# Shift transposes as 64-row pairs at the head of a unit, and V and x work kept to one whole-array stretch, in an attention and FFN kernel

## The chip, the cores and the metric

The kernel runs on one core of a Trainium2 chip. The metric is the device time of one launch in microseconds (us); several runs are given by their median. One run was also recorded by the hardware profiler, and its span, from the first to the last instruction, is what the trace describes. The engines are named as the profile names them: PE is the matrix engine and PEld its weight loads, DVE the vector engine, ACT the scalar (activation) engine, POOL the GpSimd engine, SP the queue that issues DMAs.

## What is computed

A block of attention and a feed-forward block, both between layer norms, for 2 batches of 2048 tokens with 256 features, 16 heads of 64, and 768 hidden units. All data is float32.

```python
x = x + layernorm(attn(layernorm(x)))
x = x + layernorm(ffn(layernorm(x)))

def attn(x):                       # 16 heads, K = 64
    q, k, v = x @ Wq + bq, x @ Wk + bk, x @ Wv + bv
    p = softmax(q @ k.T / sqrt(K))
    y = x + (p @ v) @ Wo + bo
    return layernorm(y, eps=1e-3) * gamma + beta

def ffn(x):                        # weights are int32, scaled by 1/127
    return (silu(x @ wg.T) * (x @ wu.T)) @ wd.T
```

## The kernel before

**Units.** The attention is cut into 64 units `(b, p, c)`: 2 batches, 8 pairs of heads, 4 chunks of 512 queries, in this order. A unit has 16 key tiles `kt` of 128 keys, taken as two blocks, j = 0 and j = 1, of 8. For a key tile, `scores` (L581) makes four pairs of matmuls; one matmul of a pair works for each head, on 64 of the array's 128 rows. The first three pairs are the product of K and Q, each split in a rounded part and a rest. The fourth pair adds the softmax's shift: `unit` times `SH[u]`, a row of 512 numbers for each head. ACT then takes the exponent (L598). So the fourth pair can't start before `SH[u]` is there.

**Where the shift comes from.** While unit u's scores run, `max_pair` (L549) computes the raw scores of the next unit, one pair of matmuls between two key tiles, and DVE reduces them to maxima. `shift_min` (L568) leaves the negated maxima, by query, in `n8`. `shift_row` (L573) turns them: four transposes on the PE, into PSUM, and one ACT copy (L579) from there to `SH[u]` in SBUF.

**A unit's order** is written out by hand in `run_unit` (L791), and each engine works through its own instructions in that order. A block is: 8 key tiles of scores; one half of an earlier unit's output projection, `wo_half` (L232), on 64-row tiles; `add_up`, which sums exponents on DVE and POOL; `advance("R")`, which gives loads, norms and casts their turn; in block j = 0 then `advance("F")`, the work that uses the whole 128 by 128 array; then `pv` (L617), 16 matmuls with V on tiles of 64 columns. In block j = 0 a sum over the exponents (`sum_up`, L188) follows, on the same 64-column tiles. In block j = 1 there follow `shift_row` of the next unit, `cs_item` (L218), and a second `advance("F")`. `cs_item` adds the two halves of P times V on DVE (`cf`, L221), rounds the result on ACT (`cs`, L223) and leaves the rest of it to POOL (L224). The four transposes of `shift_row` use the whole array.

**Work for later** is handed out by `items` (L635). A job is a generator that yields "R" or "F", the kind of turn at which it wants to go on. `now(j, ...)` puts a piece into the "F" turn of block j. The pieces that matter here are:

- `projs` (L502): one or two projections of Q or K, 6 matmuls each, read out by ACT and DVE. A unit with c = 3 has three of them.
- `v_tile` (L527): 24 matmuls that make V for 512 keys and two head pairs, read out by one DVE add (L547).
- `next_x` (L494): loads a chunk of the next batch's x, normalizes it (ACT) and transposes it (`x_item`, L483).
- the `piece` jobs of `prep_jobs` (L322): transpose 18 pieces of the FFN's weights, one for each unit from the fifth on.
- `head_job` (L269): the norms between attention and FFN for batch 0, with 8 transposes at their end.

**PSUM.** All of `scores`, `wo_half`, `shift_row`, `projs`, `v_tile`, `x_item` and the transposes of jobs take their output buffers from one ring of two, `t`. `max_pair` and `pv` share another ring of two. A buffer is taken again when its readers are done.

Of the kernel before, what the change touches and what calls it, by code (L numbers as in the profile page):

```python
# [8 lines left out]
F32 = mybir.dt.float32  # L9
# [7 lines left out]
P = 128  # L17
# [11 lines left out]
def kernel(  # L29
# [18 lines left out]
    nc = tc.nc  # L48
# [105 lines left out]
    def double():  # L154

        return banks["t"].tile([P, 2, 512], F32, tag="t", name="t")
# [165 lines left out]
    def prep_jobs():  # L322
        jobs = []

        def piece(w, dst, o, i0):
            src = hd.tile([P, TT, D], F32, tag="hx", name="wi")[:, 0, :].bitcast(I32)
            nc.sync.dma_start(out=src, in_=w[o * P : (o + 1) * P, i0 * P : (i0 + 2) * P])
            yield "R"
            f = hd.tile([P, TT, D], F32, tag="hy", name="wf")[:, 0, :]
            nc.scalar.copy(f, src)  # L330
            yield "F"
            yield "F"
            ps = double()[:, 0, :]
            for i in range(2):
                nc.tensor.transpose(ps[:, i * P : (i + 1) * P], f[:, i * P : (i + 1) * P], ident)
            t = hd.tile([P, TT, D], F32, tag="ht", name="wt")[:, :2, :].bitcast(F32R)
            split(t, ps[:, : 2 * P])
            for k in range(2):
                nc.sync.dma_start(
                    out=dst[:, k, i0 : i0 + 2, o * P : (o + 1) * P],  # L340
                    in_=f32(t[:, k, :]).rearrange("p (i n) -> p i n", i=2),
                )

        for w, dst, no, ni in (
            (w_gate, wg_dram, HC, DC),
            (w_up, wu_dram, HC, DC),
            (w_down, wd_dram, DC, HC),
        ):
            for o in range(no):
                for i0 in range(0, ni, 2):  # L350
                    jobs.append(piece(w, dst, o, i0))
        return jobs
# [36 lines left out]
    with ExitStack() as actx:  # L389
# [76 lines left out]
        def x_load(b, c):  # L466
            t = hd.tile([P, TT, D], F32, tag="ht", name="xc")
            nc.sync.dma_start(out=t, in_=x_chunk(b, c))
            return t
# [23 lines left out]

        def next_x(b, c):  # L494

            t = x_load(b, c)
            yield "R"
            x_norm(b, c, t)
            yield "F"
            x_item(c, t)  # L500
# [71 lines left out]

        def shift_row(u):  # L573

            ps = double()[:, 0, :]
            for qt in range(QT):
                nc.tensor.transpose(ps[:, qt * P : (qt + 1) * P], n8[:, qt, :], ident)  # L577
            SH[u] = bw.tile([P, QB], F32R, tag="sh", name="sh", bufs=2)
            nc.scalar.copy(SH[u], ps)  # L579

        def scores(u, kt):  # L581

# [52 lines left out]
        def items(g):  # L635

            b, p, c = units[g]
            at = {}

            def put(j, kind, f, *a, late=False):  # L640
                at.setdefault((j, kind), []).append((late, lambda: f(*a)))

            def now(j, f, *a):


                def job():
                    f(*a)
                    yield from ()

                put(j, "F", job)  # L650

            left = len(units) - g
            if p == 0:
                put(1, "R", start_acc, c)
            if b == 0 and p and prep:
                put(0, "R", lambda: prep.pop(0), late=True)
            if b == 1 and 4 * p + c in (5, 11, 17, 23):
                put(0, "R", head_job, 0, (5, 11, 17, 23).index(4 * p + c), nc.gpsimd, late=True)
            if left == 3:
                put(1, "R", load_ffn, 0)  # L660
            if left == 2:
                put(0, "R", load_ffn, 1)
                put(1, "R", load_ffn, 2)
            if left == 1:
                put(0, "R", load_ffn, 3)
            if b == 0 and p == 0:

                put(0, "R", x_stats_item, 1, c, late=True)


            want = [(0, *units[g + 2])] if left > 2 else []
            nb, npair = (b, p + 1) if p + 1 < NP else (b + 1, 0)
            if nb < B:
                same = nb == b
                want += [
                    (1, nb, npair, i)
                    for i in {1: (0,) if same else (), 2: (1,) if same else (0, 1), 3: (2, 3)}.get(c, ())
                ]
            for i in range(0, len(want), 2):
                now(0, projs, *want[i : i + 2])  # L680
            if c == 0 and p % 2 == 0:

                if g:
                    now(0, v_tile, b, p // 2, 3)
            if nb == B:
                return at
            if c == 0:
                put(0, "R", load_w, 1, nb, npair)
            if c == 1:
                put(0, "R", load_w, 0, nb, npair)  # L690
            if c == 2:
                put(0, "R", load_wo, nb, npair)
            if nb != b and c < 2:
                put(0, "R", next_x, nb, 2 * c)
                put(1, "R", next_x, nb, 2 * c + 1)
            if npair % 2 == 0:
                pg = npair // 2
                if c == 0:
                    put(1, "R", load_wv, nb, pg)
                if c == 2:  # L700
                    now(1, v_tile, nb, pg, 0)
                if c == 3:
                    now(1, v_tile, nb, pg, 1)
                    now(1, v_tile, nb, pg, 2)
            return at

        def begin():


            first = units[0]  # L710
            xs = [acc[:, c * TT : (c + 1) * TT, :] for c in range(NC)]

            def raw(tag):
                return lambda: hd.tile([P, TT, D], F32, tag=tag, name="raw").rearrange(
                    "p t d -> p (t d)"
                )[:, :512]

            ws = [load_w(0, 0, 0), load_w(1, 0, 0, raw("hx")), load_wv(0, 0, raw("hy"))]
            for c in range(NC):
                nc.sync.dma_start(out=xs[c], in_=x_chunk(0, c))  # L720
                if c < 3:
                    next(ws[c])

            def stats(c):
                ln_stats([xs[c][:, i, :] for i in range(TT)], mvx[0], c * TT)

            def rstd(c, n, eng=None):
                k = slice(c * TT, (c + n) * TT)
                ln_rstd(rsx[0][:, k], nbx[0][:, k], mvx[0][:, k, :], n * TT, LN_EPS, eng)

            def maxima(a, b):
                for i in range(a, b):
                    max_pair(first, i)

            stats(0)
            rstd(0, 1)
            drain(ws[0])
            x_norm(0, 0, xs[0])
            drain(ws[1])
            stats(1)  # L740
            rstd(1, 1, nc.gpsimd)
            stats(2)
            x_item(0, xs[0])
            x_norm(0, 1, xs[1])
            stats(3)
            rstd(2, 2, nc.gpsimd)
            projs((0, *first))
            projs((1, 0, 0, 0))
            maxima(0, 2)
            x_item(1, xs[1])  # L750
            maxima(2, 3)
            x_norm(0, 2, xs[2])
            projs((1, 0, 0, 1))
            maxima(3, 5)
            x_item(2, xs[2])
            drain(ws[2])
            x_norm(0, 3, xs[3])
            maxima(5, 6)
            projs((1, 0, 0, 2))
            maxima(6, 8)  # L760
            x_item(3, xs[3])
            maxima(8, 9)
            projs((1, 0, 0, 3))
            maxima(9, 10)
            v_tile(0, 0, 0, True)
            maxima(10, 12)
            projs((0, *units[1]))
            maxima(12, 13)
            v_tile(0, 0, 1, True)
            maxima(13, 15)  # L770
            v_tile(0, 0, 2, True)
            maxima(15, 16)
            shift_min(first)
            v_tile(0, 0, 3, True)
            shift_row(first)
            drain(load_wo(0, 0))

        running = []
# [11 lines left out]

        def run_unit(g, u):  # L791
            at = items(g)
            ahead = units[g + 1] if g + 1 < len(units) else None
            behind = units[g - 1] if g else None
            for j in range(2):
# [23 lines left out]
                if j == 0:  # L819
                    if behind:  # L820
                        sum_up(behind, pvs[u][:, 1, :])
                    first_half(u, behind)
                else:
                    if ahead:
                        shift_row(ahead)
                    cs_item(u)
                    advance("F", at.get((j, "F"), []))

        with tc.manual_schedule(engines={EV.PE, EV.DVE, EV.Activation, EV.Pool}):
            begin()  # L830
# [285 lines left out]
```

## Time and profile before

| What | us |
|---|---|
| median of 3 runs (lowest, highest) | 3004.85 (3004.0, 3007.09) |
| profiled execution, device time | 3004.34 |
| its span | 3002.6 |
| DVE busy (71%) | 2131.2 |
| ACT busy (49%) | 1473.3 |
| POOL busy (82%) | 2454.2 |

The device time is 1.74 us more than the span. The mean granted clock of the PE is 0.991 of full speed. A unit takes about 42 us; the first unit's scores begin at about 58 us, the last unit ends at about 2733 us, and the FFN follows. In the groups of the profile a line shows the source line, the engine and the operation, the tiles written and read, the shapes, and after the bar the busy time, the mean length of one in ns, and the time its engine stood idle ahead of it with what ended that. In the timeline a line is one merged stretch: start, length, engine, line, operation, tiles, count, and in brackets the idle time ahead and its releaser. Matmuls overlap each other, so the distance from one weight load to the next says more of the PE's pace than the length of a matmul.

### The profile page before, as it was taken

To read this page: it belongs to the slowest core of one execution; us is meant where nothing else is said; L and a number is where in the kernel's file an instruction comes from. 1 tells how busy PE (TensorE), PEld (TensorE's weight loads), DVE (VectorE), ACT (ScalarE), POOL (GpSimd) and SP (SyncE) were. 2 spreads that over 40 slices of the span, in tenths; PEclk is the share of its full clock that TensorE was granted. 3 is DMA by queue.
4 is the path that set the end of the run, shared out by engine and by line. 5 is a ranking of instruction groups with operands and counts; after the bars stand their busy time and mean duration, and the time that the engine had idled before them with its cause. 6 is when DMAs were issued, how large, how long until landed. Compare 5 with 4: busy or idle time off the path is not lost. (4 is left out here: it accounts for less than half of the span.)

```text
span 3002.6 us, 48405 instructions
## 1 busy us (share of the span) xinstructions
PE 2902.3 (97%) x19236; PEld 1751.5 (58%) x19236; DVE 2131.2 (71%) x2755; ACT 1473.3 (49%) x1756; POOL 2454.2 (82%) x1451
## 2 busy tenths in 40 slices
PE   7999999999999999999999999999999999999787
PEld 5555555556555665556555665556555655556666
DVE  6777667676767777766777777776777777764775
ACT  4555445444544545564545545554554545444343
POOL 4999778787878788877888998898899889996553
PEclk9999999999999999999999999999999999999989
DMA  5000000000000000010100010000001001021100
GB/s 85 19 12 13 13 14 13 14 15 13 12 15 21 15 5 6 10 40 24 27 5 4 5 39 7 1 16 30 5 5 40 4 3 36 15 69 59 43 19 25
DMA packets 127475, 61.08 MB, mean 20 GB/s; under 512 B 77264, under 2 KB 120528, under 8 KB 126864
## 3 DMA queue, kind: packets, MB, share of 16 engines
q1 hardware_dynamic: 127088, 57.72, 7.7%
q8 instruction: 150, 2.46, 0.4%
q14 instruction: 77, 0.63, 0.1%
q0 software_dynamic: 160, 0.27, 0.1%
HBM read 39.85 MB, written 17.83 MB: 19 GB/s over the span
## 5 line engine op out<-in xcount | busy, mean ns | idle before, releaser
L615 POOL TENSOR_TENSOR accs<-accs,pt 128x1024 f32<-128x1024 f32 x636 | 1623.7, 2553 | 288.0 <-ACT pt L598 242.8
L566 DVE TENSOR_REDUCE nm<-s 128x2 f32<-128x1024 f32 x1024 | 1215.1, 1225 | 495.4 <-PE s L559 495.1
L598 ACT ACTIVATE pt<-t 128x1024 f32<-128x1024 f32 x1024 | 1049.7, 1027 | 254.2 <-PE t L597 193.9
L597 PE MATMUL t<-QN,KT 64*128 64x512 f32 x6144 | 912.6, 401 | 9.4 <-DVE hn L178 5.1
L625 PE MATMUL s<-pt,v 128*64 128x512 f32 x4096 | 910.5, 597 | 0.0
L597 PEld LDWEIGHTS t<-QN,KT 64*128 64x128 f32 x6144 | 520.7, 185 | 245.0 <-ACT pt L598 170.8
L625 PEld LDWEIGHTS s<-pt,v 128*64 128x64 f32 x4096 | 283.7, 137 | 541.1 <-issue 528.8
L559 PE MATMUL s<-KT,QN 64*128 64x512 f32 x2048 | 423.5, 410 | 3.7 <-DVE cf L221 1.9
L597 PE MATMUL t<-sh,unit 64*128 64x512 f32 x2048 | 405.3, 392 | 0.0
L615 POOL TENSOR_TENSOR accs<-accs,two 128x1024 f32<-128x1024 f32 x128 | 305.0, 2383 | 19.0 <-DVE two L608 9.1
L606 DVE TENSOR_TENSOR two<-pt 128x1024 f32<-128x1024 f32 x128 | 298.1, 2329 | 0.0
L559 PEld LDWEIGHTS s<-KT,QN 64*128 64x128 f32 x2048 | 192.0, 184 | 127.1 <-issue 62.7
L214 ACT COPY rr<-s 128x1024 f32<-128x1024 f32 x63 | 63.9, 1014 | 397.6 <-PE s L190 390.4
L579 ACT CAST sh<-t 128x512 fp32r<-128x512 f32 x64 | 37.6, 587 | 413.3 <-PE t L577 413.3
L254 DVE SCALAR_TENSOR_TENSOR acc<-t,rc,acc 128x256 f32<-128x256 f32 x500 | 206.9, 477 | 19.6 <-PE t L243 12.8
L597 PEld LDWEIGHTS t<-sh,unit 64*128 64x128 f32 x2048 | 192.9, 184 | 44.8 <-ACT sh L579 0.2
L612 POOL TENSOR_TENSOR accs<-pt 128x1024 f32<-128x1024 f32 x64 | 153.6, 2401 | 49.1 <-ACT pt L598 48.9
L512 PE MATMUL t<-xh,wqk 128*128 128x512 f32 x512 | 181.5, 415 | 12.3 <-ACT pt L598 10.1
L943 POOL TENSOR_TENSOR hT<-hf,hT 128x512 fp32r<-128x512 f32 x48 | 62.0, 1291 | 103.5 <-ACT hT L942 103.4
L512 PEld LDWEIGHTS t<-xh,wqk 128*128 128x128 f32 x512 | 97.7, 191 | 47.1 <-ACT pt L598 22.9
L522 ACT ACTIVATE QN<-t,bq_sb 128x512 fp32r<-128x512 f32 x64 | 44.0, 688 | 163.9 <-PE t L512 163.9
L221 DVE TENSOR_TENSOR cf<-s,rr 128x512 f32<-128x512 f32 x64 | 44.2, 691 | 104.2 <-PE s L625 104.2
(160 smaller groups left out, 2316.2 us busy)
## 6 DMA issues: line engine op xcount, KB each, us to landing
few<-rr SPq DMA_DIRECT2D x512, 0.5 KB, 2.0
xc<-in_L_attn_x_dram SPq DMA_DIRECT2D x8, 512.0 KB, 3.9
acc<-in_L_attn_bo_dram SPq DMA_DIRECT2D x8, 512.0 KB, 8.5
xT_dram<-hn SPq DMA_DIRECT2D x16, 256.0 KB, 2.9
out_dram<-o SPq DMA_DIRECT2D x15, 256.0 KB, 2.1
xT<-xT_dram SPq DMA_DIRECT2D x3, 1024.0 KB, 5.9
attn_dram<-acc SPq DMA_DIRECT2D x5, 512.0 KB, 2.6
acc<-in_L_attn_x_dram SPq DMA_DIRECT2D x4, 512.0 KB, 7.5
```

The costliest lines, as they stand in the source:

```text
L214: nc.scalar.copy(r, ps)
L254: nc.vector.scalar_tensor_tensor(a, ps[e][:, i * D : (i + 1) * D], inv[:, e, q : q + 1], a, ALU.mult, ALU.add)
L512: nc.tensor.matmul(ps[:, k, :], w[:, wi, dc, :], xx[:, dc, s], start=n == 0, stop=n == 5)
L559: nc.tensor.matmul(s[:, e, :], QN[u][half(e), 0, qt * P : (qt + 1) * P], KT[b, p, kc][half(e), 0, :], start=True, stop=True,)
L566: nc.vector.tensor_reduce(nm[u][:, :, qt, kc : kc + 1], s, AX.X, ALU.max, negate=True)
L597: nc.tensor.matmul(ps[:, e, :], w, r, start=n == 0, stop=n == 3)
L598: nc.scalar.activation(pt, ps, AF.Exp, scale=QSCALE)
L606: nc.vector.tensor_tensor(two, p8[n], p8[n + 1], ALU.add)
L612: nc.gpsimd.tensor_tensor(accs[u], todo[0], todo[1], ALU.add)
L615: nc.gpsimd.tensor_tensor(accs[u], accs[u], t, ALU.add)
L625: nc.tensor.matmul(pvs[u][half(e), 0, :], v[:, kt % 4, n : n + K], pt[:, e, :], start=kt % 8 == 0, stop=kt % 8 == 7,)
L943: nc.gpsimd.tensor_tensor(t[:, 1], hf, f32(t[:, 0]), ALU.subtract)
```

## The change

`shift_row` moves from the end of a unit, for the next one, to the head of the unit that uses it; so in program order it now stands behind the `cs_item` of the unit before, and no longer ahead of it. Its transposes are now eight on halves of the array, one for each of the two 64-row tiles in turn, with 64 columns of the identity each; the two tiles write to the two halves (banks) of the `t` buffer, and the ACT copy puts the halves together with strided patterns. For the first unit it moves behind the load of the first `wo`.

The second "F" turn, at the end of block j = 1, is gone. What stood there goes into block j = 0: V tile 0 of the next two head pairs into the unit with c = 2, tiles 1 to 3 together into the unit with c = 0 that first uses them (tile 3 was there already), and the transposes of `next_x` and of `head_job` into the next "F" turn of a block j = 0. `next_x` uses three buffers in turn, so that two chunks can be loaded in the same turn. A weight `piece` yields "F" once, which leaves it in the same stretch as before, and except for p = 1 no piece starts in a unit with c = 2.

```diff
@@ piece @@
             yield "F"
-            yield "F"
             ps = double()[:, 0, :]
@@ next_x @@
-            t = x_load(b, c)
+            t = hd.tile([P, TT, D], F32, tag=("hx", "hy", "ht", "hx")[c], name="xc")
+            nc.sync.dma_start(out=t, in_=x_chunk(b, c))
@@ shift_row @@
-            ps = double()[:, 0, :]
+            ps = double()
             for qt in range(QT):
-                nc.tensor.transpose(ps[:, qt * P : (qt + 1) * P], n8[:, qt, :], ident)
+                for h in range(2):
+                    nc.tensor.transpose(
+                        ps[:, h, qt * K : (qt + 1) * K], n8[half(h), qt, :], ident[half(h), half(h)]
+                    )
             SH[u] = bw.tile([P, QB], F32R, tag="sh", name="sh", bufs=2)
-            nc.scalar.copy(SH[u], ps)
+            nc.scalar.copy(
+                SH[u].rearrange("p (q h r) -> p h q r", h=2, r=K),
+                ps[:, :, : QT * K].rearrange("p h (q r) -> p h q r", r=K),
+            )
@@ items (now() has no j any more: always block 0) @@
-            if b == 0 and p and prep:
+            if b == 0 and p and (c != 2 or p == 1) and prep:
...
-                if g:
-                    now(0, v_tile, b, p // 2, 3)
+                for i in range(1, 4) if g else ():
+                    now(v_tile, b, p // 2, i)
...
-                put(1, "R", next_x, nb, 2 * c + 1)
+                put(c, "R", next_x, nb, 2 * c + 1)
...
                 if c == 2:
-                    now(1, v_tile, nb, pg, 0)
-                if c == 3:
-                    now(1, v_tile, nb, pg, 1)
-                    now(1, v_tile, nb, pg, 2)
+                    now(v_tile, nb, pg, 0)
@@ begin @@
             v_tile(0, 0, 3, True)
-            shift_row(first)
             drain(load_wo(0, 0))
@@ run_unit @@
             at = items(g)
+            shift_row(u)
...
                 else:
-                    if ahead:
-                        shift_row(ahead)
                     cs_item(u)
-                    advance("F", at.get((j, "F"), []))
```

More of the change, by code (lines that the diff above doesn't have):

```diff
@@ L641, in put, with now @@
                 at.setdefault((j, kind), []).append((late, lambda: f(*a)))
-            def now(j, f, *a):
+            def now(f, *a):
                 def job():
@@ L648, in job @@
                     yield from ()
-                put(j, "F", job)
+                put(0, "F", job)
             left = len(units) - g
@@ L679, in items @@
             for i in range(0, len(want), 2):
-                now(0, projs, *want[i : i + 2])
+                now(projs, *want[i : i + 2])
             if c == 0 and p % 2 == 0:
-                if g:
-                    now(0, v_tile, b, p // 2, 3)
+                for i in range(1, 4) if g else ():
+                    now(v_tile, b, p // 2, i)
             if nb == B:
```

## The prediction, made before the changed kernel ran

> **What bounds the kernel now.** I read the page's busy times and slices first, then the groups, then the timeline of one seam between two units, then the list of waits.
>
> ```profile
> span 3002.6 us, 48405 instructions
> PE 2902.3 (97%) x19236; PEld 1751.5 (58%) x19236; DVE 2131.2 (71%) x2755; ACT 1473.3 (49%) x1756; POOL 2454.2 (82%) x1451
> PE   7999999999999999999999999999999999999787
> ...
> L221 DVE TENSOR_TENSOR cf<-s,rr 128x512 f32<-128x512 f32 x64 | 44.2, 691 | 104.2 <-PE s L625 104.2
> ```
>
> The PE is full in every slice of the attention, so the question is what an edit does to the PE's queue. The last line says that DVE stands idle ahead of `cf` until the PE has finished `pv`. So `cf` can't come sooner.
>
> This is an ordinary seam, from the last `pv` to the second exponent:
>
> ```profile
> 768.90 0.42 PEld L577 LDWEIGHTS t<-ident,n 128*128 128x128 f32 x4 [0.81 <-issue]
> 769.02 0.69 DVE L221 TENSOR_TENSOR cf<-s,rr 128x512 f32<-128x512 f32 x1 [1.73 <-PE s L625]
> 769.49 0.19 PEld L559 LDWEIGHTS s<-KT,QN 64*128 64x128 f32 x2 [0.17 <-issue]
> ...
> 769.59 0.65 PEld L597 LDWEIGHTS t<-QN,KT 64*128 64x128 f32 x6
> 769.59 0.59 ACT L579 CAST sh<-t 128x512 fp32r<-128x512 f32 x1 [6.94 <-PE t L577]
> ...
> 770.08 0.62 ACT L223 CAST cs<-cf 128x512 fp32r<-128x512 f32 x1
> 770.28 0.19 PEld L597 LDWEIGHTS t<-sh,unit 64*128 64x128 f32 x2
> ...
> 771.01 2.18 ACT L598 ACTIVATE pt<-t 128x1024 f32<-128x1024 f32 x2 [0.31 <-PE t L597]
> ...
> 772.08 0.53 PEld L597 LDWEIGHTS t<-QN,KT 64*128 64x128 f32 x6 [0.22 <-ACT pt L598]
> ```
>
> The shift's copy starts at 769.59, as soon as the transposes are done, ends at 770.18, and the pair that needs it (770.28) hasn't waited: its weight load follows the one before (769.59 + 0.65) by 0.04. The copy fits into one max pair and three score pairs with 0.1 us to spare. ACT does `sh` first and `cs` second, as the program has them.
>
> One seam shows how fast `cf` is followed by `cs` when ACT has nothing else to do (0.04 us):
>
> ```profile
> 1987.52 0.68 DVE L221 TENSOR_TENSOR cf<-s,rr 128x512 f32<-128x512 f32 x1
> ...
> 1988.24 0.62 ACT L223 CAST cs<-cf 128x512 fp32r<-128x512 f32 x1 [2.14 <-DVE cf L221]
> 1988.26 0.19 PEld L559 LDWEIGHTS s<-KT,QN 64*128 64x128 f32 x2 [1.87 <-DVE cf L221]
> ```
>
> And these waits belong to what the change moves:
>
> ```profile
> PEld t L335 <- DVE KT L523: 9.3, 4, 2.6
> PEld t L597 <- DVE v L547: 2.5, 14, 0.3
> PE t L335 <- DVE KT L523: 7.6, 4, 2.1
> PE t L597 <- DVE hn L178: 5.1, 4, 1.4
> ```
>
> [...] 0.81 us without a weight load after `pv`, 0.17 us between the transposes and the 64-row max pair. [...] Here the copies of 512 take 587 (`sh`) and 623 ns (`cs`), and `cs` starts 0.49 us after `sh` with 0.587 us of length, an overlap of 0.10.
>
> **Part 1, `shift_row` behind `cs_item`.** On the PE nothing gets later: [...] The whole-array to 64-row drain of 0.17 us goes. Eight half transposes in four pairs stand for four whole ones, which took 0.42 us. The trace has no such pair; the nearest row is `wo_half`, six pairs of 64-row tiles with weight loads 0.12 us apart, so about 0.47 us. Bounds: [...] 1.1 us if the eight run one by one at the 0.14 us of one weight load. None of these decides, because of the ACT queue. ACT meets `cs` first, which waits for `cf`, which waits for the end of `pv`; `sh` stands behind it, and behind `sh` the first exponent. From the first transpose at T = 0:
>
> - `cf` on DVE: 0.12 to 0.81 (as before)
> - `cs` on ACT: 0.81 + 0.04 = 0.85
> - `sh` on ACT: 0.49 later, 1.34, ends 1.34 + 0.59 = 1.93
> - weight load of the pair with `sh`: 0.04 later (exponent to weight load, 772.04 to 772.08), 1.97
>
> Before it was 770.28 - 768.90 = 1.38. So each seam loses 0.59 us, and the time saved on the transposes lies inside this wait: without the wait the pair would come at about 1.24. Queued behind the waiting pair on the PE are the next max pair and all scores after it, so DVE's maxima and ACT's exponents slide along. It isn't won back within the block: a buffer of the `t` ring comes round by exponent 1.03, hand-over 0.05, four pairs and hand-over 1.24 more, 2.37 for two key tiles (771.01, 773.38, 775.75), and the PE alone needs 10 pairs at the 0.2325 us between their weight loads, 2.33. The strided copy could cost more than 587 ns; the `cs` cast's 623 would add 2 us in all, 0.1 us each 6 us. 63 seams x 0.59 = **+37.2**.
>
> Two seams (1987.5 and 2325.6) have a late `cf`, held up by DVE's norms. There the PE now waits for `cf` at the second max pair, at 1988.26. With the change that pair comes at 1988.20 + 0.04 + 0.49 + 0.59 + 0.04 + 0.23 = 1989.59, 1.33 later instead of 0.59: **+1.5** for both. The first unit's copy waits for the cast of `wo` (0.42): **+0.3**.
>
> **Part 2, V tiles.** 24 matmuls at 0.117 us spacing are 2.82 us wherever they stand; 21 of the 28 V tiles move, for nothing in sum. At c = 0 three stand in a row: tile 2 needs the buffer of the Q projection, whose DVE part ended at 742.49 in the trace while tile 1 would run to 742.98, and tile 3 needs tile 1's, read out by 744.5 against 745.8. No wait. V tile 1 is first used at `pv` 4, microseconds later. The 14 seams that had V tiles in them lose their DVE collision: from the first max pair to `wo_half` such a block takes 736.99 - 727.12 = 9.87, an ordinary one 779.21 - 769.49 = 9.72. 14 x 0.15 = **-2.1**.
>
> **Part 3, weight pieces.** Four pieces in c = 3 stretches waited for a buffer until DVE had read out K (PE idle 1.67, 2.13, 1.68, 2.13 in the timeline). Three (p = 2, 3, 4) go elsewhere: **-5.9**. But in c = 2 with p = 1, 3, 5 a piece now stands behind a V tile and takes the buffer of the projections. In an equal stretch the projections ended at 783.05; a V tile would end at 785.87, K was read out at 786.96: 3 x 1.1 = **+3.3**.
>
> **Part 4, x and heads.** `next_x` loads two chunks at once; SP issues four DMAs as before, a turn earlier at most, and ACT does 8 norms ahead of one seam, where it was idle for 5.27 us with four of them (2.06 us) done. Two x transposes now follow each other in a stretch, and the projection behind needs the buffer whose DVE part waits for `two`: about 2 us more PE wait in one stretch, and in the next, with two projections and a V tile behind, some 4 more, against 1.35 each at the old seams and 1.2 each for norms that are now ready or no longer alone. I take **+1.6**, bounds -3 and +5. The heads lose their 5.1 us behind `hn`, and two of four (c = 3) now wait like a piece, 2 x 2.1: **-0.9**.
>
> Sum: 37.2 + 1.5 + 0.3 - 2.1 - 5.9 + 3.3 + 1.6 - 0.9 = +35.0. Span 3002.6 + 35.0 = 3037.6; with the 1.74 outside the span 3039.3; the median stood 0.5 above the profiled run, so 3039.8, said as 3039.5.
>
> **Rivals.**
>
> - *The drain decides (faster).* If ACT has `sh` done in time, because `cs` doesn't stand ahead of it in its queue, the seams gain 1.38 - 1.24 = 0.14 each, 8.8, and parts 2 to 4 give 4.0: 3004.85 - 12.8 = 2992. For it: two mode changes fewer in every seam. Against: ACT kept the written order in every seam I read, and DVE idles ahead of `cf` in 60 of 64. It decides if the pair with `sh` comes before 1.38.
> - *Half absorbed.* The block catches up, if a delayed start lets the ring run at the PE's own 2.33 for two tiles instead of 2.37: 16 tiles x 0.02 = 0.3 a unit, so 63 x 0.29 = 18 instead of 37: 3021. Against: the ring's period is made of latencies that the delay leaves alone.
> - *More than computed.* A strided copy or slow pairs make `sh` 0.15 to 0.2 later still: 63 x 0.17 = 11, 3050.
> - *It does nothing.* The waits cancel: only by chance.
>
> **Numbers.** Forecast 0.68; half absorbed 0.12; more 0.10; faster 0.08; within 0.2% (6 us, about what a measurement of this kernel can tell from no change) 0.02. The likeliest case alone spans 3031 to 3046 (parts 3 and 4 and the copy's length); the range 3017 to 3050 takes in the half-absorbed case and most of the costlier one. Faster 0.08, same 0.03, slower 0.89.
>
> **What would show it.** In the changed trace: ACT's order at each seam `cs`, then `sh`, with `cs` starting 0.04 us behind the end of `cf` and `sh` without idle time ahead of it; a wait of the weight load with `sh` on ACT's `sh` 63 times, about 0.7 us each; the pieces' wait on K gone from three c = 3 stretches; V tiles three in a row without idle PE. I'm wrong if the pair with `sh` follows the third pair without a gap.

## The result, and the profile after

The changed kernel takes 3035.44 us (median of 4 runs, 3033.93 to 3036.34), the kernel before 3005.06 in the same session: 1.01 times the time, with a 95% interval of 1.0082 to 1.0117. The profiled run has a span of 3034.0 us, 31.4 more than before. The prediction was 3039.5.

From the page of the changed kernel, the span, the busy times and three groups of instructions:

```profile
span 3034.0 us, 48913 instructions
PE 2898.0 (96%) x19492; PEld 1740.2 (57%) x19492; DVE 2121.2 (70%) x2755; ACT 1475.4 (49%) x1756; POOL 2453.8 (81%) x1451
...
L603 PE MATMUL t<-sh,unit 64*128 64x512 f32 x2048 | 410.8, 398 | 36.0 <-ACT sh L582 36.0
...
L223 ACT CAST cs<-cf 128x512 fp32r<-128x512 f32 x64 | 39.7, 620 | 435.0 <-DVE cf L221 435.0
L221 DVE TENSOR_TENSOR cf<-s,rr 128x512 f32<-128x512 f32 x64 | 44.2, 691 | 107.3 <-PE s L631 107.3
```

No engine has noticeably more to do: ACT is busy 2.1 us longer, and the PE's busy time is even 4.3 us shorter. But the matmul with `sh` now waits, and it waits for ACT. The list of waits of the same kernel (operation, releaser: total us, times, longest) says how often:

```profile
ACT cs L223 <- DVE cf L221: 435.0, 64, 8.3
...
PEld t L603 <- ACT sh L582: 63.8, 64, 2.0
PE t L603 <- ACT sh L582: 36.0, 63, 1.6
```

ACT itself waits 64 times ahead of `cs`, and the PE 63 times for `sh`, 36.0 / 63 = 0.57 us each. The timeline of the seam that the prediction showed, in the changed kernel:

```profile
772.27 0.32 PEld L578 LDWEIGHTS t<-ident,n 64*128 64x128 f32 x8 [0.81 <-issue]
772.38 0.69 DVE L221 TENSOR_TENSOR cf<-s,rr 128x512 f32<-128x512 f32 x1 [1.75 <-PE s L631]
772.51 0.20 PEld L559 LDWEIGHTS s<-KT,QN 64*128 64x128 f32 x2
...
773.11 0.62 ACT L223 CAST cs<-cf 128x512 fp32r<-128x512 f32 x1 [7.08 <-DVE cf L221]
773.64 0.58 ACT L582 CAST sh<-t 128x512 fp32r<-128x512 f32 x1
774.26 0.19 PEld L603 LDWEIGHTS t<-sh,unit 64*128 64x128 f32 x2 [0.98 <-ACT sh L582]
774.27 0.50 PE L603 MATMUL t<-sh,unit 64*128 64x512 f32 x2 [0.55 <-ACT sh L582]
...
774.60 0.39 PE L559 MATMUL s<-KT,QN 64*128 64x512 f32 x2
```

The reader is to see the order on ACT: `cs` first, because the program has it first, and `sh` without idle time behind it, although its transposes were done more than half a microsecond before. The max pair after the one with `sh` comes 774.60 - 772.27 = 2.33 us after the first transpose. In the kernel before it came at 770.74, 1.84 us after its first transpose at 768.90:

```profile
770.51 0.40 PE L597 MATMUL t<-sh,unit 64*128 64x512 f32 x2
770.74 0.40 PE L559 MATMUL s<-KT,QN 64*128 64x512 f32 x2
```

The two overlap, 770.51 + 0.40 against 770.74. The seam loses 0.49 us.

To see where the rest goes I cut both traces at the first transpose of each of the 64 seams and compared the 63 distances between them. Unit numbers count from 0 through both batches. Up to the last seam the changed kernel is 27.0 us behind:

| part of the difference, after minus before | us |
|---|---|
| every seam +0.50 (ordinary units: 0.47 to 0.52) | 63 x 0.50 = +31.5 |
| first seam, start | +1.1 |
| V tiles, no longer across 14 seams | about -2.1 |
| three pieces (units with c = 3 and p = 2, 3, 4) | -10.6 |
| pieces behind V tile 0 (c = 2, p = 1, 3, 5) | about +1.5 |
| the two x units (p = 7, c = 1 and 2) | +6.7 |
| heads, late `cf` | -1.2 |
| sum | +26.9 |

The other 4.4 us come after the last seam. 3.2 of them lie in the FFN, where the granted clock of the PE was 0.85 between 2948.7 and 2972 in this run and 1.00 in the corresponding stretch before. No edit touches that stretch. A PE wait of 2.4 us stands ahead of it in both kernels (2934.85 before, 2963.10 after), and only in the changed one does the clock halve behind it (0.50 for 6.8 us from 2963.21). Whether that is chance isn't shown.

Two rows of the table, the pieces and the x units, are much larger than their waits, and both have the same thing in them. These are three windows of the kernel before, behind the piece of unit 11 (columns: busy time of PE, PEld, DVE, ACT, POOL, then PEclk, DMA share, GB/s). The stretch begins with a PE that has stood idle for 2.13 us:

```profile
526.94 0.44 PE L335 MATMUL t<-ident,wf 128*128 128x128 f32 x2 [2.13 <-DVE KT L523]
```

```profile
526.00:527.00 1.00, 0.06 (x1) 0.06 (x2) 0.86 (x2) 0.68 (x2) 0.92 (x1) 1.00 0.00 0
528.00:529.00 1.00, 1.00 (x4) 0.24 (x2) 0.25 (x1) 0.00 (x0) 1.00 (x1) 0.50 0.29 89
...
532.00:533.00 1.00, 1.00 (x8) 0.36 (x6) 0.00 (x0) 0.00 (x0) 0.00 (x0) 1.00 0.00 0
```

A microsecond after the wait the granted clock falls to 0.50 and stays there for 3.4 us, while the PE is called fully busy and starts four matmuls in a microsecond instead of eight. Half the clock for 3.4 us costs 1.7 us. The kernel before has two such windows in its attention, behind the two pieces that waited 2.13 us, and none behind the two that waited 1.67 and 1.68. The changed kernel has none there, but three windows' worth (5.1 us at most, for in the first microsecond of it the PE still waited) in the two x units:

```profile
1336.02 0.80 PE L512 MATMUL t<-xh,wqk 128*128 128x512 f32 x1 [1.94 <-DVE xl L491]
```

```profile
1336.00:1337.00 1.00, 0.98 (x2) 0.83 (x3) 1.00 (x1) 0.00 (x0) 1.00 (x1) 0.50 0.75 267
```

They stand at waits of 2.03 us (ahead of the matmul at 1290.33) and 1.94. The last section has what the two traces show of the idle time ahead of such windows.

### The profile page after: what moved, and what is told of

It reads as the page before. It is cut to its first block, busy times and chain, and to the rows that moved or that the text cites. A ratio compares the mean times of both kernels' runs of the same rounds, so it can differ in the third digit from the quotient of the medians.

```text
span 3034.0 us, 48913 instructions
## 1 busy us (share of the span) xinstructions
PE 2898.0 (96%) x19492; PEld 1740.2 (57%) x19492; DVE 2121.2 (70%) x2755; ACT 1475.4 (49%) x1756; POOL 2453.8 (81%) x1451
## 5 line engine op out<-in xcount | busy, mean ns | idle before, releaser
L612 DVE TENSOR_TENSOR two<-pt 128x1024 f32<-128x1024 f32 x128 | 276.4, 2159 | 0.0
L603 PEld LDWEIGHTS t<-sh,unit 64*128 64x128 f32 x2048 | 192.4, 184 | 107.1 <-ACT sh L582 63.8
L223 ACT CAST cs<-cf 128x512 fp32r<-128x512 f32 x64 | 39.7, 620 | 435.0 <-DVE cf L221 435.0
```

What stands on the lines that cost most here:

```text
L603: nc.tensor.matmul(ps[:, e, :], w, r, start=n == 0, stop=n == 3)
L612: nc.vector.tensor_tensor(two, p8[n], p8[n + 1], ALU.add)
```

## The experiments

My theory: the whole seam loss comes from the place of the `sh` copy on ACT, behind `cs`, and the moved work is a second, smaller thing. The rivals: the 64-row transposes with the strided copy cost the time, or the moved V, x and pieces do. "Seams" in what follows are read from ordinary units, against the kernel before. All ratios are against runs of the kernel before on the same chip.

**1. `sh` back ahead of `cs`, the rest as changed**

```diff
@@ run_unit, on the changed kernel; the first unit's shift_row goes back to begin @@
-            shift_row(u)
...
+                    if ahead:
+                        shift_row(ahead)
                     cs_item(u)
```

> The changed kernel, but shift_row for the next unit is issued at the end of block j = 1 ahead of cs_item (no other work stands between it and the next unit's scores), so that ACT does sh first and cs second. Theory (sh waits in ACT's queue behind cs): the pair with sh follows the third pair without a gap, about 1.3 us after the first transpose instead of 2.0; each of 63 seams gets 0.79 us shorter (second max pair at 1.54 instead of 2.33), so 50 us less, about 2985 us, below the kernel before by 20. Rival (the pair form, its strided copy or the work moved to block j = 0 cost the time): it stays near 3035.

2998.45 us, ratio 0.9966 (0.9953 to 0.9979). The timeline of the same seam:

```profile
760.11 0.33 PEld L578 LDWEIGHTS t<-ident,n 64*128 64x128 f32 x8 [0.81 <-issue]
...
760.61 0.59 ACT L582 CAST sh<-t 128x512 fp32r<-128x512 f32 x1 [6.78 <-PE t L578]
...
761.10 0.62 ACT L223 CAST cs<-cf 128x512 fp32r<-128x512 f32 x1
761.26 0.19 PEld L603 LDWEIGHTS t<-sh,unit 64*128 64x128 f32 x2
761.39 0.41 PE L603 MATMUL t<-sh,unit 64*128 64x512 f32 x2
761.63 0.40 PE L559 MATMUL s<-KT,QN 64*128 64x512 f32 x2
```

Moving one line turns ACT's order round. `sh` ends at 761.20, the pair with it follows the pair before without a gap, and the max pair after it comes 1.52 us after the first transpose, against 2.33 in the changed kernel and 1.84 before. Ordinary units are 0.30 shorter than before and 0.80 shorter than changed. So the pair form is a gain once nothing hides it, and the order on ACT alone makes it a loss. I missed the total by 13 us on the low side: the moved work took it. The two x units cost 7.8 more than the seams explain, unit 54 with its neighbours 5.9.

**2. The kernel before, with `shift_row` at the unit's head only**

```diff
@@ run_unit, on the kernel before; the first unit's shift_row goes from begin @@
+            shift_row(u)
...
-                    if ahead:
-                        shift_row(ahead)
                     cs_item(u)
                     advance("F", at.get((j, "F"), []))
```

> The kernel before, with only the place of shift_row changed: whole-array transposes at the head of the unit, behind cs_item and behind the second F turn, which stays. Theory: the 43 seams without whole-array work lose about 0.49 us each, 21 us; in the 20 seams with a V tile, x or head transposes between, cf and cs run under that work and sh is not late: 3026 us in all. Rival (the place of sh costs nothing, the moved V and x work does): 3005.

3033.44 us, ratio 1.0082 (1.0065 to 1.0098): nothing else of the change is in it, and it costs as much as the whole change. Ordinary units are 0.50 longer. I had expected the 20 seams with V, x or head work in them to be spared. They weren't: three units of a V group together lost 1.42, 3 x 0.47. At such a seam (341 us in this kernel) the last matmul of the V tile starts at 341.00 and the transposes follow it at 341.12, without a wait. What waits is the first pair of the scores behind them, at 342.40, and it waits for the end of `sh`:

```profile
342.40 0.50 PE L597 MATMUL t<-QN,KT 64*128 64x512 f32 x2 [0.24 <-ACT sh L579]
```

13 of the 14 seams with V tiles show this wait, of 0.24 or 0.25; only at the fourteenth do the transposes wait for the V tile's readout, 0.45 us. That the scores wait because the V tile and the transposes hold both buffers of the ring `t` fits, but wasn't tried.

**3. The changed kernel with the old transposes**

```diff
@@ shift_row, on the changed kernel @@
-            ps = double()
+            ps = double()[:, 0, :]
             for qt in range(QT):
...
+                nc.tensor.transpose(ps[:, qt * P : (qt + 1) * P], n8[:, qt, :], ident)
...
+            nc.scalar.copy(SH[u], ps)
```

> The changed kernel with the four whole-array transposes and the plain copy of before in shift_row, at the same place. Theory: the transposes lie under the wait for sh, so nothing changes: 3035 us, within 4. Rival (pairs or the strided copy cost time): some 6 us less, 3029 or below. Rival (pairs save a drain at every seam that is felt): 63 x 0.3 more, about 3054.

3036.25 us, ratio 1.0095 (1.008 to 1.011): the same as the change, and ordinary units again 0.50 longer. With `sh` behind `cs` the form of the transposes is worth nothing, in either direction. The strided copy takes 579 ns in the changed kernel, and so does the plain one here; ahead of `cs` they take 588 (kernel 1) and 587 (before). So the 8 ns belong to the place and not to the strides.

**4. The moved work alone: old `shift_row`, in its old place, with the new places of V, x, heads and pieces**

> The kernel before in its shift_row (whole array, ahead of cs_item at the end of the unit), with V, x, heads and pieces moved to block j = 0 as in the changed kernel. Theory: the moved work alone gives what the trace leaves when the 63 seams are taken off, about -5 us: 3000 us. Rival (the moved work costs the time): 3015 or more.

3022.03 us, ratio 1.0046 (1.0031 to 1.0061), where I had expected a gain. Its edit is the diff of the change without its `shift_row` parts. Ordinary units are as before (within 0.05). At the last seam it is 14.0 us behind: the pieces gain 10.5, but the x units cost 7.8, unit 54 and its neighbours 4.0, units 56 to 59 4.1, units 40 to 47 5.1, and pieces behind a V tile about 1 each. Counted over every microsecond of the attention with a granted clock below 0.97, the clock lost it 13.6 us, against 3.4 before.

Unit 54 shows a wait that I hadn't seen coming. From the timeline of this kernel, SP's queue, then DVE, then the PE:

```profile
2318.57 0.33 SPq L450 DMA_DIRECT2D raw_w<-in_L_attn_Wo_dram  x1
2318.99 0.86 SPq L318 DMA_DIRECT2D xT_dram<-hn  x2
2322.11 0.32 SPq L289 DMA_DIRECT2D hy<-attn_dram  x1
2322.52 2.87 SPq L199 DMA_DIRECT2D few<-rr  x3
```

```profile
2330.14 0.20 DVE L229 RECIPROCAL rc<-few 128x8 f32<-128x8 f32 x1 [7.66 <-DMA few<-rr]
```

```profile
2332.16 1.65 PE L597 MATMUL t<-QN,KT 64*128 64x512 f32 x6 [2.40 <-DVE acc L254]
```

The transfer of the softmax sums (`few`) stands last in SP's queue: behind a load of Wo that waits for its buffer, behind the second pair of the head's stores, and behind the head's next load. In the kernel before the head's stores had gone out at 2294.93 and the sums at 2312.90. DVE gets the sums late, the output is late, and the PE stands still for 2.40 us.

Why the moved work costs 14.0 here and gains 4.5 under the changed kernel's slower seams (27.0 - 31.5) isn't settled. Of the 18.5 between them, 8.5 lie in half-clock windows (13.6 against 5.1). A longer unit gives POOL and SP more slack, which fits but is argued. Part of it is chance: kernel 3, whose x work and heads are those of the changed kernel, spent 3.9 less on the x units and 3.8 more on units 53 to 55. Kernel 5 too spent 3.5 more on the latter, so the profiled run of the changed kernel was a lucky one there.

**5. The changed kernel with x spread over four units**

```diff
@@ items, on the changed kernel @@
-            if nb != b and c < 2:
-                put(0, "R", next_x, nb, 2 * c)
-                put(c, "R", next_x, nb, 2 * c + 1)
+            if b + 1 < B and 26 <= 4 * p + c < 30:
+                put(0, "R", next_x, b + 1, 4 * p + c - 26)
```

> The changed kernel, but the four x chunks of the next batch are loaded one a unit, in the units 26 to 29, and transposed one a unit in the next unit's whole-array stretch, normalized a block earlier. Theory (two x transposes in a row wait for DVE and let the clock fall): the 6.7 us that units 29 and 30 lost beyond seams and V, and the waits that x had in the kernel before, go: about 3025 us. Rival (the seams alone decide): 3035.

3029.26 us, ratio 1.0073 (1.0056 to 1.009). Units 27 to 30 together are 6.0 shorter, and the mean granted clock of the profiled run is 0.992, against 0.990 in the changed kernel. Two x chunks in one stretch, with their waits and the clock behind these, cost what the table says.

**6. Both repairs: 1 and 5 together**

> e1 (sh ahead of cs in ACT's queue, pair form) with the x chunks spread over four units. Theory: the 63 seams give 0.3 us each, 19 us, and x some 13 us less than in e1: 2985 us, 20 below the kernel before. Rival (x costs as much wherever it stands): as e1, 2998.

2989.34 us, ratio 0.9943 (0.9928 to 0.9957), faster than the kernel before. The two gains add up: against the changed kernel's 1.01 they are 0.013 and 0.003.

**7. The changed kernel with a longer queue on ACT**

```diff
@@ shift_row, on the changed kernel @@
+            more = op.tile([P, QB // 2], F32, tag="more", name="more")
+            nc.scalar.copy(more, ps[:, 0, : QB // 2])
             SH[u] = bw.tile([P, QB], F32R, tag="sh", name="sh", bufs=2)
```

> The changed kernel with one more ACT copy, of 256 elements a partition, ahead of sh in each seam (its output is not used). Theory: ACT's queue is the path of every seam, so its 0.31 us (0.40 less the overlap of 0.09) appear 63 times: 19 us more, 3055. Rival (the first pair is held by something else, ACT has room): 3035.

3059.63 us, ratio 1.0174 (1.0159 to 1.019). The expected 0.40 is near the 396 ns of the casts of 256 elements in the kernel before (L428), and 0.09 is the overlap of `cs` and `sh` at the seam above (773.11 + 0.62 - 773.64). The added copy takes 365 ns and overlaps its neighbours by some 0.1. Ordinary units lose 0.77 instead of 0.50: 0.27 more, 63 x 0.27 = 17. The list of waits has, in place of the 36.0 of the changed kernel,

```profile
PE t L605 <- ACT sh L584: 55.7, 63, 3.2
```

So the time that the copy adds on ACT ahead of `sh`, 0.365 less 0.1, goes into the unit one to one. At the last seam it is 23.0 behind the changed kernel; the other 6 are mixed: units 53 to 59 cost 9.9 more, the x units 4.2 less, and 3.4 more went to half-clock windows somewhere among them.

**8, 10 and 11. Kernel 6 with the head jobs at other units**

```diff
@@ items, on kernel 6; the line behind it has the same numbers @@
-            if b == 1 and 4 * p + c in (5, 11, 17, 23):
+            if b == 1 and 4 * p + c in (4, 11, 18, 25):    # kernel 8
+            if b == 1 and 4 * p + c in (1, 9, 17, 25):     # kernel 10
+            if b == 1 and 4 * p + c in (5, 13, 21, 26):    # kernel 11
```

> e6 with the head jobs begun at units 4, 11, 18 and 25 of the second batch instead of 5, 11, 17 and 23, so that a head's last stores and the next head's load stand further apart in SP's queue. Theory: the sums of unit 54 no longer land late behind them (in e1 that unit lost about 6 us), so 2980 us. Rival (the sums are late for another reason): 2985, as e6.

> e6 with the head jobs begun at units 1, 9, 17 and 25 of the second batch, so that the transposes of every head fall into a unit with c = 1, which has one projection pair and no V tile, and four units pass between one head's end and the next head's load. Theory (heads cost where they meet V, three projections, or the next head's load ahead of the sums in SP's queue): some 8 us below e6, 2981 us, and unit 54 takes about 42.5 instead of 49.2. Rival (the sums' DMAs are late anyway): 2989.

> e6 with the head jobs begun at units 5, 13, 21 and 26 of the second batch: their transposes fall into c = 1 with even p three times and into c = 2 of the last head pair once, where no V tile is made. Theory (a head in c = 1 of an odd p makes the sums late, because there SP's queue stands behind a load of Wo that waits for POOL's work on wv, and the head's stores are issued behind it and ahead of the sums): no unit behind a head takes over 43 us, unit 54 about 42.5 instead of 49.2, in all 2981 us. Rival (a head in c = 1 makes them late in any p, as in three of the four of the run before): 2997 or more.

Kernel 8: 2984.56 us, ratio 0.9925 (0.991 to 0.9939). Its theory failed in the main: unit 54 still took 47.6 us (49.2 in kernel 6), and from the first seam to the last the two traces differ by 3.2 us only. Kernel 10: 2998.65, 0.9976 (0.9968 to 0.9984), a miss: units 38, 46 and 54 now took 49 to 50 us, each with late sums behind a head. From that came the theory that 11 tried. In pairs with odd p, the load of Wo waits for its buffer, and a head's stores in the unit before queue up behind it, so heads belong into even p. Kernel 11: 2984.79, 0.9939 (0.9922 to 0.9956). Lists of waits, first of kernel 6, then of kernel 10, then of kernel 11:

```profile
DVE rc L229 <- DMA few<-rr: 21.2, 4, 10.2
```

```profile
DVE rc L229 <- DMA few<-rr: 30.2, 5, 8.9
```

```profile
DVE rc L229 <- DMA few<-rr: 6.9, 2, 6.2
```

DVE's wait for the sums falls from 21.2 to 6.9 (not all of it was lost time: the kernel before has 17.8), and unit 54 takes 42.6 us instead of 49.2. Kernels 8 and 11 are the fastest of the study, 21 to 22 us below the kernel before, and can't be told apart.

**9. The kernel before with one condition on the pieces**

```diff
@@ items, on the kernel before @@
-            if b == 0 and p and prep:
+            if b == 0 and p and (c != 2 or p == 1) and prep:
```

> The kernel before with one edit: no weight piece starts in a unit with c = 2 except for p = 1 (pieces otherwise wait for K's readout in c = 3, PE idle 2.13, 1.68 and 2.13 us). Theory (an idle PE of about 2 us costs a window at half clock besides): both half-clock windows (528 to 531.4 and 869 to 872.4) that matter here, the ones of p = 2 and p = 4, go with the waits, so about 5.9 + 2 x 1.7 = 9.3 and some of the pieces' own switching: 2995 us. Rival (only the wait itself is lost): 2999.

2995.64 us, ratio 0.9971 (0.9961 to 0.9981), as expected. Units 11, 15 and 19 are 4.23, 2.14 and 4.26 us shorter, and the mean granted clock of the profiled run is 0.994, against 0.991 before. The two that gain 4.2 are those that have a window of half clock in the kernel before: 2.13 of wait, 1.7 of clock and 0.4 that I can't name. This part of the change was good by itself.

## Why the prediction was right, and where it was off

**The direction and the cause were right.** ACT takes `cs` first, `sh` directly behind it, and the PE waits for it 63 times. Kernels 1 and 2 put the cause in one place from both sides: put back, the loss turns into a gain of 0.30 a seam; moved alone, it costs as much as the whole change. Kernel 7 adds that a longer queue on ACT lengthens the unit by the same amount. Of the signs that the prediction named, the weight load with `sh` waits for ACT at every seam, but 1.00 us (63.8 / 64) and not 0.7.

**The largest term was too large, 37.2 for 31.5.** The weight load of the pair with `sh` came 1.99 us after the first transpose, where 1.97 was computed. The step that was off is the comparison with the kernel before. There I took the weight load at 770.28. But that load ran ahead of its matmul, which started only at 770.51, and 0.23 of its earliness was worth nothing. In the changed kernel the matmul follows its load within 0.01 us (774.26 and 774.27), but then takes 0.33 to the next pair instead of 0.23. From pair to pair, the max pair behind `sh`, the seam loses 2.33 - 1.84 = 0.49. That is 63 x 0.50 = 31.5, 5.7 less than computed.

**The transposes** were computed at about 0.47 us from the nearest row. They took 0.24 from the first weight load to the max pair's, against 0.59 for four whole ones with the 0.17 without a weight load behind them. As predicted, none of it counts under the wait (kernel 3). Without the wait the seam gains 0.30 (kernel 1), where the rival "the drain decides" had put 0.14. What the prediction calls drains and mode changes are stretches without a weight load, 0.81 and 0.17 us in the kernel before; in the changed one the 0.81 is still there and the 0.17 isn't. What the array does in them wasn't shown.

**"Half absorbed" fell:** ordinary units are 0.47 to 0.52 longer, and the ring gave nothing back. So did "more than computed": the copy with strides took as long as the plain one.

**V tiles:** -2.1 was computed at 0.15 each, and units that lose a collision and nothing else of weight show 0.07 to 0.20. Right.

**Pieces:** -5.9 was computed and -10.6 measured. The waits were right; the term left out the clock, 2 x 1.7, which no step of the prediction had. The other 1.3 of the difference have no name yet. The pieces behind a V tile cost 0.5 each and not 1.1.

**x:** +1.6 was computed with bounds of -3 and +5, and +6.7 measured, beyond the bounds. Up to 5.1 of it is half clock, and without that some 1.6 remain. That this equals the term is in part luck: the waits of the PE grew from 4.2 to 7.2 us, by 3.0, where the prediction had 5.1 and 6. The half clock at the waits of 2.03 and 1.94 us was missing again, with the other sign.

**Heads, late `cf` and the start:** +0.9 was computed (+1.5, -0.9 and +0.3) and about -0.1 measured (-1.2 and +1.1). In the changed kernel this is small. In kernels 1, 4 and 6, whose seams are shorter, the place of a head in SP's queue costs 4 to 6 us at unit 54 alone; the prediction looked at SP for x only.

In sum the terms that are off go -5.7 (seams), -4.7 - 1.8 (pieces), +5.1 (x) and -1.0 (heads and start), together -8.1, and the FFN's clock with what lies around it gave +4.4 back. The time came out 4 us under the prediction. That the sum came this close is luck, for its errors of 1 to 6.5 us have both signs; the direction is not.

## What to carry to other kernels

A small copy that many instructions wait for belongs ahead, in its engine's queue, of anything that waits longer than it does: here `sh` behind the waiting `cs` kept the PE waiting 0.57 us at each of 63 seams, and one line decided between +0.50 and -0.30 us a seam. When a delay is computed from a trace, compare the start of the same matmul, not of its weight load, for a load that ran ahead has slack (0.23 us here). A job that is moved takes its DMAs along, so look at every queue it passes, and at the clock behind an idle PE: behind two waits of 2.13 us it cost 1.7 us more than their length, behind two of 1.67 and 1.68 nothing.

## What was unexpected of the hardware

The granted clock halved at PE waits of about 2 us: behind the two of 2.13 in the kernel before, behind the one of 2.03 and within the one of 1.94 in the changed kernel. In the attention such windows lost 3.4 us in the kernel before, 5.1 in the changed one and 13.6 in kernel 4, always in steps of 1.7, so the same work can differ by some microseconds between runs (3.9 on the x units between kernel 3 and the changed kernel). None of the 63 waits of 0.57 us at the seams was followed by one.

The length of a wait alone didn't decide. These two, in the FFN of the kernel before and of the changed one, are equally long, and only the second has half clock behind it:

```profile
2934.85 0.33 PE L917 MATMUL misc<-ident,acc 128*128 128x128 f32 x1 [2.42 <-ACT acc L131]
```

```profile
2963.10 2.80 PE L917 MATMUL misc<-ident,acc 128*128 128x128 f32 x8 [2.43 <-ACT acc L131]
```

Their place differs. In each of the two traces the half-clock windows start on one grid of 3.413 us, to within 1 ns. The first wait lies across a line of this grid (1.93 us of it in one window, the rest in the next), the second inside one window. I counted the idle time of the PE in every window of the grid, over these two traces from the 60th us on. Of the 18 windows at full clock with 1.87 us or more of idle PE, 17 were followed by half clock; of the 1687 with less, none. The one exception is the window with 1.93, while one with 1.88 in each trace (from 865.88 before, from 1331.64 in the changed kernel) was followed by half clock. So in these two traces half clock went with the idle time within one window in all but one case; why the 1.93 was spared stays open, and none of this was tried with an edit.

Transposes in pairs on 64-row tiles were twice as fast as expected, 0.24 us for eight against 0.47, and a copy that reads PSUM and writes SBUF with strides was no slower than a plain one at the same place, 579 ns each.
